# Keys by seven block products for two groups at a time, query products in front of the outputs, one probability buffer

## The chip, the cores and the metric

The kernel runs on one core of a Trainium2 chip. The metric is device time in microseconds (us) of one execution. Five engines work side by side, each with its own instruction queue: TensorE (PE) multiplies matrices into the accumulators (PSUM, 8 banks of 128 x 512 float32), VectorE (DVE) and ScalarE (ACT) do arithmetic and can read PSUM, GpSimd (POOL) does arithmetic on the working memory, and SyncE (SP) issues the transfers (DMA).

## The reference

Four sequences of 256 tokens, 512 features each, go through a half-weighted gated network, causal attention over a window of 128 tokens, and the same half-weighted network again:

```python
x = x + 0.5 * ffn(layernorm(x))
x = x + attention(layernorm(x))
x = x + 0.5 * ffn(layernorm(x))

def attention(x):                       # 32 query heads, 8 key heads, 128 wide
    q = rope(x @ wq); k = rope(x @ wk); v = x @ wv
    scores = q @ k.T / sqrt(128), only where (j <= i) & (j > i - 128)
    return (softmax(scores) @ v) @ wo   # four query heads share one key head
```

`ffn` is a 512 x 512 base product plus the outputs of the best two of eight small experts (16 wide). All is float32.

## The kernel before

**Halves, groups, units.** The 1024 tokens are treated in two halves `h` of two sequences (512 tokens). In each half the attention loop runs over eight groups `g`, one key head with its four query heads, and in each group over the two sequences `b`. One pass `(h, g, b)` is called a unit; there are 32. The loop is software-pipelined: in a unit the outputs of the unit before are formed, the transposes and values of this unit, the scores of the next unit, and keys, queries and values for the next group (or pair of groups).

**Products by blocks.** Queries (`queries`) and outputs (`outputs`) are not plain products. The weights and the tokens are cut into two by two blocks, some sums of blocks are made beforehand, and seven block products take the place of eight, with some additions after them. The names `a11` ... `s4` are blocks and sums on one side, `b11` ... `t4` on the other. `sums_a` and `sums_b` make them on POOL (four operations each; some in place), `sum_weights` for the query weights `wqs`, `sum_o_weights` for the output weights `wos`, `outputs` for the attention result `oTs`. `sum_tokens` makes the sums `xs` of the normalized tokens `xa` on DVE, once in a half. In `queries` every product fills one PSUM bank (two times 256 columns, two matmuls each); products 2, 3 and 4 add to banks that 1, 5 and 7 left. The sums between them (`p1c` copied by ACT, `u2`, `v1` and the sums into banks by DVE) use tiles with one slot each.

**Keys and values.** `keys` computes one group's keys by `project`: four matmuls of 512 columns (all tokens of the half) into one bank, and then `rope`, which is three DVE products and one POOL addition. `project_v` makes the values of two groups together, one tile of 128 tokens in a unit.

**Scores and probabilities.** `scores` puts the scores of one unit into three banks and takes the maxima on DVE; `exponentials` runs eight exponentials on ACT into a buffer `probs[b]`, one of two; `normalize` divides on POOL; `transposes` brings the probabilities into the layout that `values` multiplies with.

**PSUM.** Two tags with four banks each: "mm" for queries, keys, values, outputs and attention results, "s" for scores and transposes.

**The order.** A planner orders the instructions of PE, DVE and SP: it prefers the order in which they are written, but takes a later one where an earlier one, by its own estimate, isn't ready. From line 703 on, POOL and ACT keep the written order exactly. Every wait between engines is set by the framework, from the tiles that instructions read and write and the slots that they need.

**One unit as written** (loop from line 708): keys of the next group if b = 1; a tile of values; `normalize`; the outputs of the unit before (`late`, products in the order 4, 1 and 6, 2 and 3, 7 and 5, one bank for each); if b = 0 `sum_o_weights` and the first six steps of the next group's queries, if b = 1 `sum_weights` for the group after; `transposes`; the last two steps of the queries; the scores of the next unit; `values`; the exponentials of the next unit; and the four token sums of `outputs` for this unit. The loads of `load_qk` (keys double-buffered, queries in one slot) are written behind the queries. The table `loose` drops steps of the second network into the last eight units of the loop.

## Time and profile before

| what | value |
|---|---|
| median of 3 runs | 792.85 us (792.47 to 793.61) |
| the profiled execution | 793.98 us; its span 792.3 us, granted TensorE clock 1.000 |
| one group, two units, in the middle of a half (297.0 to 339.4) | 42.4 us; busy: PE 42.40, PEld 34.18, DVE 25.60, ACT 10.37, POOL 26.31 |
| `L374`, keys: matmuls | 128 records of 128x512, 57.5 us busy |
| `L400`, queries: matmuls | 896 records of 128x256 in four groups of rows |
| `L581`, outputs: matmuls | 868 records of 128x256 |
| POOL `L114` 128x256 / 128x512 | 738 ns / 1272 ns |
| DVE `L597` 128x256 / 128x512 out of PSUM | 405 ns / 691 ns |
| load of `wk` for one group | 256 KB, 2.7 us to landing, 16 of them |

PE and PEld are TensorE's matmuls and its weight loads, which overlap. A row of a timeline gives the start, the length, the engine and line, what is written from what, the shape, and how many instructions are merged. A row of waits gives who waited for whom, the total, how many times and the longest. Float32 matmuls leave two records each.

### The profile page before, as it was taken

To read this page: it belongs to the slowest core of one execution; us is meant where nothing else is said; L and a number is where in the kernel's file an instruction comes from. 1 tells how busy PE (TensorE), PEld (TensorE's weight loads), DVE (VectorE), ACT (ScalarE), POOL (GpSimd) and SP (SyncE) were. 2 spreads that over 40 slices of the span, in tenths; PEclk is the share of its full clock that TensorE was granted. 3 is DMA by queue.
4 is the path that set the end of the run, shared out by engine and by line. 5 is a ranking of instruction groups with operands and counts; after the bars stand their busy time and mean duration, and the time that the engine had idled before them with its cause. 6 is when DMAs were issued, how large, how long until landed. Compare 5 with 4: busy or idle time off the path is not lost.

```text
span 792.3 us, 10145 instructions
## 1 busy us (share of the span) xinstructions
PE 780.0 (98%) x3524; PEld 602.6 (76%) x3524; DVE 486.6 (61%) x1226; ACT 222.1 (28%) x766; POOL 451.4 (57%) x461
## 2 busy tenths in 40 slices
PE   6999999999999999999999999999999999999998
PEld 4557878787878888787878787878788787877654
DVE  4558563838474756659487728484757557574663
ACT  4342333222213140312222232213141412223331
POOL 5421775674747474757575665747474756653521
PEclk9999999999999999999999999999999999999999
DMA  8400221212021302112121212020303021100001
GB/s 294 158 1 19 76 67 53 93 54 67 8 99 41 106 14 91 57 53 67 54 95 53 67 54 88 23 95 9 106 14 101 20 58 49 54 1 26 1 27 54
DMA packets 33555, 48.90 MB, mean 62 GB/s; under 512 B 1248, under 2 KB 14304, under 8 KB 33504
## 3 DMA queue, kind: packets, MB, share of 16 engines
q1 hardware_dynamic: 33504, 48.26, 18.6%
q8 instruction: 28, 0.46, 0.2%
q14 instruction: 23, 0.19, 0.1%
HBM read 46.15 MB, written 2.10 MB: 61 GB/s over the span
## 4 chain that ended last, share of the span: by engine, by line
PE 96%; DMA 1%; DVE 1%; ACT 1%; SPq 0%; POOL 0%; issue 0%; DVEq 0%; ACTq 0%
PE q L400 24%; PE y L581 23%; PE pv L465 7%; PE ob L555 7%; PE pp_k L374 7%; PE po_f L330 6%; PE sb L497 5%; PE sa L482 4%; PE t L533 4%; PE oa L555 3%; PE pa_f L317 2%; PE po_f L342 1%; DMA x<-in_x_dram 1%; PE y L620 1%; PE pt_f L246 1%; ACT probs L515 0%
## 5 line engine op out<-in xcount | busy, mean ns | idle before, releaser
L369 POOL TENSOR_TENSOR qT<-ra_q,rb_q 128x512 f32<-128x512 f32 x64 | 81.4, 1272 | 154.9 <-DVE rb_q L365 154.9
L581 PE MATMUL y<-wo,oT 128*128 128x256 f32 x368 | 94.8, 379 | 0.0
L365 DVE TENSOR_TENSOR rb_q<-q,sin_sb 64x512 f32<-64x512 f32 x128 | 88.1, 688 | 1.7
L597 DVE TENSOR_TENSOR x<-y,x 128x256 f32<-128x256 f32 (+1 forms) x62 | 34.0, 548 | 83.0 <-PE y L581 82.9
L114 POOL TENSOR_TENSOR oTs<-oT 128x256 f32<-128x256 f32 x62 | 45.8, 738 | 59.7 <-ACT oT L558 57.2
L581 PEld LDWEIGHTS y<-wo,oT 128*128 128x128 f32 x368 | 69.8, 190 | 9.4
L537 ACT COPY p<-t 128x512 f32<-128x512 f32 x32 | 18.8, 586 | 203.1 <-PE t L533 203.1
L524 POOL TENSOR_TENSOR probs<-probs,sm 128x512 f32<-128x512 f32 x64 | 66.2, 1055 | 1.2 <-DVE sm L519 1.2
L581 PE MATMUL y<-wos,oTs 128*128 128x256 f32 x248 | 63.9, 380 | 0.6 <-POOL oTs L114 0.6
L465 PEld LDWEIGHTS pv<-wv,xa 128*128 128x128 f32 x256 | 48.6, 190 | 18.1 <-issue 12.9
L400 PE MATMUL q<-xa,wq 128*128 128x256 f32 x256 | 60.8, 379 | 0.0
L400 PE MATMUL q<-xs,wqs 128*128 128x256 f32 x256 | 60.6, 379 | 0.0
L400 PE MATMUL q<-xs,wq 128*128 128x256 f32 x256 | 60.5, 379 | 0.0
L555 PE MATMUL ob<-p,v 128*128 128x512 f32 x128 | 60.1, 592 | 0.0
L465 PE MATMUL pv<-wv,xa 128*128 128x256 f32 x256 | 60.0, 379 | 0.0
L330 PE MATMUL po_f<-wb_sb,xn_f 128*128 128x512 f32 x128 | 57.9, 594 | 0.0
L374 PE MATMUL pp_k<-xa,wk 128*128 128x512 f32 x128 | 57.5, 592 | 0.0
L590 DVE TENSOR_TENSOR z<-y,z 128x512 f32<-128x512 f32 x46 | 31.7, 690 | 40.2 <-PE y L581 40.2
L515 ACT ACTIVATE probs<-probs,nm 128x64 f32<-128x64 f32 (+1 forms) x128 | 46.3, 364 | 35.7 <-DVE nm L511 30.2
L400 PEld LDWEIGHTS q<-xa,wq 128*128 128x128 f32 x256 | 48.5, 190 | 6.9 <-issue 0.2
L400 PEld LDWEIGHTS q<-xs,wqs 128*128 128x128 f32 x256 | 48.6, 190 | 6.6
L581 PEld LDWEIGHTS y<-wos,oTs 128*128 128x128 f32 x248 | 46.9, 190 | 7.5 <-POOL oTs L114 1.0
(142 smaller groups left out, 1489.2 us busy)
## 6 DMA issues: line engine op xcount, KB each, us to landing
wq<-in_wq_dram SPq DMA_DIRECT2D x16, 1024.0 KB, 5.4
wo<-in_wo_dram SPq DMA_DIRECT2D x16, 1024.0 KB, 5.3
wk<-in_wk_dram SPq DMA_DIRECT2D x16, 256.0 KB, 2.7
wv<-in_wv_dram SPq DMA_DIRECT2D x8, 512.0 KB, 3.5
x<-in_x_dram SPq DMA_DIRECT2D x8, 256.0 KB, 7.2
out_dram<-x SPq DMA_DIRECT2D x8, 256.0 KB, 2.0
wb_sb<-in_w_base_dram SPq DMA_DIRECT2D x1, 1024.0 KB, 7.8
ar_sb<-in_w_ar_dram SPq DMA_DIRECT2D x1, 272.0 KB, 4.8
```

Of the source, the lines that this page charges most:

```text
L114: nc.gpsimd.tensor_tensor(dst, p, q, op)
L330: nc.tensor.matmul(po[i], x_of(i, c), wb_sb[:, c, :], start=(c == 0), stop=False)
L365: nc.vector.tensor_tensor(twice(b[o : o + half, :]), twice(src[i : i + half, :]), angle(sin_sb[o : o + half, :]), ALU.mult,)
L369: nc.gpsimd.tensor_tensor(dst, view(a), view(b), ALU.add)
L374: nc.tensor.matmul(pp, w[:, c, :], xa[h][:, c, :], start=(c == 0), stop=(c == KC - 1))
L400: nc.tensor.matmul(bank[:, ts(j, S)], w[:, c, ts(j, HD)], x[:, c, :], start=(new and j == 0 and c == 0), stop=(c == 1), skip_group_check=True,
L465: nc.tensor.matmul(pv[:, : 2 * HD], xa[h][:, c, ts(i, P)], weights["v", h, g][:, c, :], start=(c == 0), stop=(c == KC - 1),)
L497: nc.tensor.matmul(pb[:, ts(e, 3 * BLK)], q[:, 2 + e, 2 * p : 2 * p + 2, :], k[:, n - P : n + BLK], start=True, stop=True,)
L515: nc.scalar.activation(pr[:, n, :keys_of], src[:, :keys_of], AF.Exp, bias=nm[:, n : n + 1], scale=scale, accum_out=sm[:, n : n + 1],)
L524: nc.gpsimd.tensor_tensor(w, w, sm[:, n : n + G].unsqueeze(2).to_broadcast([P, G, P]), ALU.mult)
L555: nc.tensor.matmul(po, v[:, 2 * b + n, cols], part, start=(n == 0), stop=(n == len(parts) - 1))
L581: nc.tensor.matmul(py[:, ts(i, D // 2)], lhs[n - 1][:, c, :], weights["os", h, g][n - 1][:, c, :], start=(i == 0 and c == 0), stop=(c == 1 ...
```

## The change

`load_qk` is cut in two. `load_k` loads the key weights of two groups (512 KB) into one slot, `load_q` the queries' as before. `sum_weights` gets a kind, and makes block sums of key weights too. `keys` computes the keys of groups g and g + 1 at once: the rows of blocks are the two heads, the columns the two sequences, so that block c11 is head g for the first sequence, c12 head g for the second, and c21 and c22 are head g + 1. Two banks hold the four blocks, two blocks in each. It is called in the prologue for groups 0 and 1, and then in every second b = 1 unit. In a b = 0 unit all eight query steps are written in front of the outputs of the unit before; keys too now stand behind the values' tile and in front of the outputs. `probs` is one buffer. The loads change places as shown.

```diff
@@ -88,12 +88,18 @@
 
     weights = {}
 
-    def load_qk(h, g):
-        wk_g = sb.tile([P, KC, HD], F32, tag="wk", name=f"wk_{h}_{g}")
-        nc.sync.dma_start(out=wk_g, in_=wk[:, ts(g, HD)].rearrange("(c p) f -> p c f", p=P))
+    def load_k(h, g):
+
+        wk_g = sb.tile([P, KC, 2 * HD], F32, tag="wk", bufs=1, name=f"wk_{h}_{g}")
+        nc.sync.dma_start(
+            out=wk_g, in_=wk[:, ts(g // 2, 2 * HD)].rearrange("(c p) f -> p c f", p=P)
+        )
+        weights["k", h, g] = wk_g
+
+    def load_q(h, g):
         wq_g = sb.tile([P, KC, G * HD], F32, tag="wq", bufs=1, name=f"wq_{h}_{g}")
         nc.sync.dma_start(out=wq_g, in_=wq[:, ts(g, G * HD)].rearrange("(c p) f -> p c f", p=P))
-        weights["k", h, g], weights["q", h, g] = wk_g, wq_g
+        weights["q", h, g] = wq_g
 
     def load_v(h, g):
         wv_g = sb.tile([P, KC, 2 * HD], F32, tag="wv", name=f"wv_{h}_{g}")
@@ -119,13 +125,14 @@
             nc.gpsimd.tensor_tensor(dst, p, q, ALU.subtract)
         return b11, b21, b22, t4, t1, t2, t3
 
-    def sum_weights(h, g):
-
-        w = weights["q", h, g]
-        new = sb.tile([P, 3, 2, 2 * HD], F32, tag="wqs", bufs=1, name=f"wqs_{h}_{g}")
-        weights["qs", h, g] = sums_a(
-            w[:, :2, : 2 * HD], w[:, 2:, : 2 * HD], w[:, :2, 2 * HD :], w[:, 2:, 2 * HD :],
-            *(new[:, i] for i in range(3)),
+    def sum_weights(kind, h, g):
+
+
+        w = weights[kind, h, g]
+        n = w.shape[-1] // 2
+        new = sb.tile([P, 3, 2, n], F32, tag=f"w{kind}s", bufs=1, name=f"w{kind}s_{h}_{g}")
+        weights[kind + "s", h, g] = sums_a(
+            w[:, :2, :n], w[:, 2:, :n], w[:, :2, n:], w[:, 2:, n:], *(new[:, i] for i in range(3))
         )
 
     def load_o(h, g):
@@ -189,10 +196,8 @@
     by_heads(pick, fill_pick)
 
 
-    probs = []
-    for n in range(2):
-        probs.append(const.tile([P, 2 * G, P], F32, name=f"probs{n}"))
-        nc.gpsimd.memset(probs[n][:, :G:2, BLK:], 0.0)
+    probs = const.tile([P, 2 * G, P], F32, name="probs")
+    nc.gpsimd.memset(probs[:, :G:2, BLK:], 0.0)
     picked = pick.bitcast(mybir.dt.int32).rearrange("p (c k) -> p c k", k=BLK)
 
 
@@ -368,12 +373,6 @@
             )
         nc.gpsimd.tensor_tensor(dst, view(a), view(b), ALU.add)
 
-    def project(dst, w, h, name):
-        pp = mm_bank(f"pp_{name}")
-        for c in range(KC):
-            nc.tensor.matmul(pp, w[:, c, :], xa[h][:, c, :], start=(c == 0), stop=(c == KC - 1))
-        rope(dst, pp, name)
-
     def sum_tokens(h):
 
         sums = sb.tile([P, 4, 2, S], F32, tag="xs", bufs=1, name=f"xs_{h}")
@@ -382,6 +381,12 @@
         for dst, p, q in ((t1, b12, b11), (t2, b22, t1), (t3, b22, b12), (t4, b21, t2)):
             nc.vector.tensor_tensor(dst, p, q, ALU.subtract)
         xs[h] = (b11, b21, b22, t4, t1, t2, t3)
+
+    def add(dst, bank, other):
+        nc.vector.tensor_tensor(dst, bank, other, ALU.add)
+
+    def temp(name, at):
+        return sb.tile([HD, TH], F32, tag=name, bufs=1, name=f"{name}_{at}")
 
     def queries(h, g):
 
@@ -403,29 +408,23 @@
                     )
             return bank
 
-        def temp(name):
-            return sb.tile([HD, TH], F32, tag=name, bufs=1, name=f"{name}_{h}_{g}")
-
         def turn(b, j, src):
             rope(
                 qT[h, g][:, b, :, j : j + 2, :], src, f"q_{h}_{g}_{b}_{j}",
                 lambda t: t.rearrange("p (j e q) -> p e j q", j=2, q=BLK),
             )
 
-        def add(dst, bank, other):
-            nc.vector.tensor_tensor(dst, bank, other, ALU.add)
-
         def first():
             state["p1"] = product(1)
-            state["p1c"] = temp("p1c")
+            state["p1c"] = temp("p1c", f"q_{h}_{g}")
             nc.scalar.copy(state["p1c"], state["p1"])
 
         def sixth():
-            state["p6"], state["u2"] = product(6), temp("u2")
+            state["p6"], state["u2"] = product(6), temp("u2", f"q_{h}_{g}")
             add(state["u2"], state["p6"], state["p1c"])
 
         def fifth():
-            state["p5"], state["v1"] = product(5), temp("v1")
+            state["p5"], state["v1"] = product(5), temp("v1", f"q_{h}_{g}")
             add(state["v1"], state["p5"], state["u2"])
 
 
@@ -453,8 +452,36 @@
         return [first, sixth, fifth, seventh, second, third, turn_third, fourth]
 
     def keys(h, g):
-        kT[h, g] = sb.tile([HD, TH], F32, tag="kT", name=f"kT_{h}_{g}")
-        project(kT[h, g], weights["k", h, g], h, f"k_{h}_{g}")
+
+        x, w = xs[h], weights["ks", h, g]
+        banks = [mm_bank(f"k{n}_{h}_{g}").rearrange("p (b s) -> p b s", b=BPH) for n in range(2)]
+        (c11, c12), (c21, c22) = ((bank[:, 0, :], bank[:, 1, :]) for bank in banks)
+        p1c, u2, v1 = (temp(n, f"k_{h}_{g}")[:, :S] for n in ("p1c", "u2", "v1"))
+
+        def product(n, dst, start=False):
+            for c in range(2):
+                nc.tensor.matmul(
+                    dst, w[n - 1][:, c, :], x[n - 1][:, c, :],
+                    start=(start and c == 0), stop=(c == 1), skip_group_check=True,
+                )
+
+        for i in range(2):
+            kT[h, g + i] = sb.tile([HD, TH], F32, tag="kT", name=f"kT_{h}_{g + i}")
+        product(1, c11, True)
+        nc.scalar.copy(p1c, c11)
+        product(6, c22, True)
+        add(u2, c22, p1c)
+        product(5, c12)
+        add(v1, c12, u2)
+        product(7, c21)
+        add(c22, c21, v1)
+        product(2, c11)
+        product(3, c12)
+        add(c12, c12, u2)
+        rope(kT[h, g], banks[0].rearrange("p b s -> p (b s)"), f"k_{h}_{g}")
+        product(4, c21)
+        add(c21, c21, u2)
+        rope(kT[h, g + 1], banks[1].rearrange("p b s -> p (b s)"), f"k_{h}_{g + 1}")
 
     def project_v(h, g, i):
 
@@ -472,7 +499,7 @@
     def scores(h, g, b):
         o = b * S
         q, k = qT[h, g][:, b], kT[h, g]
-        pr = probs[b]
+        pr = probs
         mx = sb.tile([P, 2 * G], F32, tag="mx", bufs=3, name=f"mx_{h}_{g}_{b}")
         sm = sb.tile([P, 2 * G], F32, tag="sm", bufs=3, name=f"sm_{h}_{g}_{b}")
         pa = score_bank(f"sa_{h}_{g}_{b}").rearrange("p (c k) -> p c k", k=P)
@@ -625,7 +652,8 @@
 
     groups = [(h, g) for h in range(NHALF) for g in range(NKV)]
     units = [(h, g, b) for h, g in groups for b in range(BPH)]
-    load_qk(*groups[0])
+    load_k(*groups[0])
+    load_q(*groups[0])
     load_v(*groups[0])
     load_o(*groups[0])
     xa = [None] * NHALF
@@ -666,17 +694,18 @@
             halves[h](step)
     norm_attn(behind.popleft())
     sum_tokens(0)
-    sum_weights(*groups[0])
+    sum_weights("k", *groups[0])
+    sum_weights("q", *groups[0])
     keys(*groups[0])
+    load_k(*groups[2])
     for step in queries(*groups[0]):
         step()
-    load_qk(*groups[1])
-    sum_weights(*groups[1])
+    load_q(*groups[1])
+    sum_weights("q", *groups[1])
     for i in range(TPH):
         project_v(0, 0, i)
     load_v(*groups[2])
     load_o(*groups[1])
-
 
 
 
@@ -708,37 +737,37 @@
     for u, (h, g, b) in enumerate(units):
         n = groups.index((h, g)) + 1
         left = len(units) - u
-        rest = []
-        if b == 1 and n < len(groups):
-            keys(*groups[n])
         at = n + n % 2
         if at < len(groups):
             project_v(*groups[at], 2 * (1 - n % 2) + b)
         normalize(ahead[0], ahead[2])
         fill(left, 0)
+        if b == 0 and n < len(groups):
+            for step in queries(*groups[n]):
+                step()
+            if n % 2 == 0:
+                sum_weights("k", *groups[n])
+        elif b == 1 and n % 2 == 0 and n < len(groups):
+            keys(*groups[n])
+            if n + 2 < len(groups):
+                load_k(*groups[n + 2])
         run(late, len(late))
         if b == 0:
             sum_o_weights(h, g)
-            if n < len(groups):
-                if n > 1:
-                    load_o(*groups[n])
-                rest = queries(*groups[n])
-                while len(rest) > 2:
-                    rest.pop(0)()
+            if n + 1 < len(groups):
+                load_q(*groups[n + 1])
+            if 1 < n < len(groups):
+                load_o(*groups[n])
         else:
             if g == NKV - 2 and h + 1 < NHALF:
                 sum_tokens(h + 1)
             if n + 1 < len(groups):
-                sum_weights(*groups[n + 1])
+                sum_weights("q", *groups[n + 1])
                 if n % 2 == 0 and n + 2 < len(groups):
                     load_v(*groups[n + 2])
         fill(left, 1)
         p0, p1 = transposes(h, g, b, ahead[0])
-        for step in rest:
-            step()
         fill(left, 2)
-        if b == 0 and n + 1 < len(groups):
-            load_qk(*groups[n + 1])
         if left > 1:
             ahead = scores(*units[u + 1])
         oT = values(h, g, b, p0, p1)
```

## The prediction

> **What bounds the kernel.** I read the page's busy times first, then its chain of waits, then the waits of TensorE alone, then TensorE's timeline through one group.
>
> ```profile
> PE 780.0 (98%) x3524; PEld 602.6 (76%) x3524; DVE 486.6 (61%) x1226; ACT 222.1 (28%) x766; POOL 451.4 (57%) x461
> ...
> PE 96%; DMA 1%; DVE 1%; ACT 1%; SPq 0%; POOL 0%; issue 0%; DVEq 0%; ACTq 0%
> ```
>
> TensorE (PE) holds 96% of the chain that ended last. Its waits (us in total, times, longest) come to 8.3 us, 7.5 of them at tile transposes, nearly all in one wait of 6.4:
>
> ```profile
> PE pt_f L246 <- ACT xc_f L235: 7.5, 2, 6.4
> PE y L581 <- POOL oTs L114: 0.6, 1, 0.6
> PE po_f L342 <- ACT ht_f L338: 0.2, 1, 0.2
> ```
>
> So in the group loop PE never stops: a matmul taken out of its stream is saved in full, and a stall put into it is paid in full. The timeline (start, length, count at the end) of one b = 1 unit:
>
> ```profile
> 315.21 1.02 PE L555 MATMUL oa<-p,v 128*128 128x512 f32 x2
> 316.07 1.88 PE L555 MATMUL ob<-p,v 128*128 128x512 f32 x4
> 317.79 3.60 PE L374 MATMUL pp_k<-xa,wk 128*128 128x512 f32 x8
> 321.22 1.89 PE L465 MATMUL pv<-wv,xa 128*128 128x256 f32 x8
> 322.95 1.03 PE L581 MATMUL y<-wos,oT 128*128 128x256 f32 x4
> 323.81 1.03 PE L581 MATMUL y<-wo,oT 128*128 128x256 f32 x4
> ```
>
> Read starts, not lengths (ends are modelled). Each float32 matmul leaves two records. Eight of 512 columns take 321.22 − 317.79 = 3.43 us, 0.429 each; eight of 256 columns take 1.73 us, 0.216 each. Half the columns cost half, plus 1.5 ns.
>
> **1. The products.** Two groups of keys take 16 records × 0.429 = 6.86 us now. The seven products are 7 × 2 matmuls × 2 = 28 records × 0.216 = 6.05 us. Gain 0.81 us a pair, and 8 pairs: **−6.5 us**.
> A rule speaks against this: the Trainium skill, "Trainium Kernel Development and Optimization", Performance Expectations, judges TensorE by weight-load busy time, not by matmul busy time. The change adds 12 loads a pair, 96 × 0.190 = 18 us, so PEld goes from 76% to about 79%. If that load were exposed, the sum would be +11.7 us. The row decides: a load of 190 ns already lies under each 256-column record spaced 216 ns apart, so I count it at nothing; only 26 ns of cover is left.
>
> **2. New side work a pair.** POOL: four 128x256 sums (row L114, 738 ns), 3.0 us. DVE: five 128x256 adds from PSUM (row L597, 405 ns), 2.0 us. ACT: one 128x256 copy (row L469, 368 ns). Over 8 pairs that is 24, 16 and 3 us, on engines busy 57, 61 and 28%: nothing by itself. What counts is where PE waits for it.
>
> **3. Unit lengths.** Take a unit's first pv matmul as 0. By the timeline's steps pv is 1.73, queries 7 × 1.73 = 12.1, outputs 6.05, transposes 0.87, scores 2.2, values 2.6. In the new order a b = 0 unit is 25.5 us: pv, queries to 13.8, outputs to 19.9, transposes to 20.7. A b = 1 unit is 13.4 us without keys, and 19.5 with them (next group even).
>
> **4. Does the key chain stall PE?** Each product must be answered in the 0.86 us of the next one: 0.2 us from PE to DVE or ACT (y ending near 337.23, its add starting at 337.43), 0.4 for the add, 0.1 back. That fits if the engine is free. ACT isn't:
>
> ```profile
> 335.32 0.35 ACT L515 ACTIVATE probs<-probs,nm 128x64 f32<-128x64 f32 x1
> ...
> 338.04 0.20 ACT L515 ACTIVATION_READ_ACCUMULATOR probs<-sb,nm 128x1 f32 x1
> 338.13 0.37 ACT L469 COPY v<-pv 128x256 f32<-128x256 f32 x1
> ```
>
> This unit began at 334.64, so exponentials hold ACT to 3.5 and the pv copy to 3.9. ACT keeps written order, so the key chain's first copy ends near 4.3. The fifth product would start at 1.73 + 2 × 0.86 = 3.45; it writes the other half of the bank that this copy reads. The Trainium skill, "PSUM — Partial Sum Buffer", section "PSUM bank collisions raise a hardware error", says to guard PSUM by bank, not by address. By address nothing waits: 0. By bank the wait is 0.85 us × 7 pairs in the loop = 6.0 us, nearly the whole gain. No row shows two engines on halves of one bank. I take the bank rule, but expect the planner to put other matmuls into the hole (the raw output products, 0.86 us each, are ready). It does such things now: near the end it moved transposes ahead of the last output products, leaving under 0.1 us:
>
> ```profile
> 749.87 1.03 PE L581 MATMUL y<-wo,oTs 128*128 128x256 f32 x4
> 750.73 1.04 PE L533 MATMUL t<-ident,probs 128*128 128x128 f32 x8
> 751.68 1.13 PE L581 MATMUL y<-wos,oTs 128*128 128x256 f32 x4
> ```
>
> Cost between 0 and 6.0, taken near 0.
>
> **5. Queries in front of outputs.** All four "mm" banks hold query sums, and outputs now follow at once (today transposes stand before the last product, scores after it). DVE frees the banks. Measured on the timeline from the first query product (300.06): adds start at 3.7, 5.4 and 7.1, ropes run 7.9 to 12.2, then both adds of u2 in 1.3 us. Today the masks push these back; in the new order they follow directly, and the last two ropes (2.1 us each) end at 15.5 and 17.7. Output banks are wanted at 12.1, 13.0, 14.7 and 16.4. The third gets its bank 1.0 us late, the fourth then 0.4 late: up to 1.4 × 14 loop units = 19 us. Movable work lies next: transposes (0.87), then scores (0.89). I take 1 us for the whole loop here. What makes up for it: the rope backlog now drains under the outputs rather than under the masks and maxima that follow transposes (today DVE gets to the scores at 318.86, 3.7 us after PE ended them).
>
> **6. POOL order.** `sum_o_weights` starts when the outputs release `wos`: today at 7.8 in a b = 0 unit, then at 19.9 to 20.9. It takes 4 × 1.345 = 5.4 us, ending at most 0.8 into the next unit, where outputs need it at 1.7 in a unit without keys. Then come four sums of 0.80 each, as now (335.50 to 338.6), so product 6 keeps the thin margin that it has today before b = 0 outputs. Normalization ends at about 6.1 (340.65 − 334.64); transposes now come at 7.8 without the keys as a cushion. Margins of 1 us and 1.7 us: nothing, but if outputs slip by another 1 us, product 6 waits some 0.6 in 8 units. Where `sum_weights("k")` lies in front (3.2 us), the next unit has 6 us of keys as cover.
>
> **7. One probability buffer.** Its writers wait for the transposes of the last unit, which already stand before scores in PE's order: 0. It removes an option, no wait.
>
> **8. Loads.** SP issues half as many key loads of twice the size, freed by the keys, wanted over one unit (25 us) later against 2.7 to 3.5 us to land. The query load moves ahead of the output load, which stands behind outputs now ending 12 us later; landing at about 27, it is wanted a unit later. 0.
>
> **9. The first group.** Keys now need DVE answers at 60 to 67 us, when DVE has half 1's updates and statistics; the query chain shares one-slot temporaries (p1c, u2, v1) with it and follows only after the last key add. Between −0.5 (earlier ropes) and +3; PE still has the query products and transposes to fill with, so +1.0.
>
> **Sum.** −6.5 + 1.0 + 1.0 = −4.5 us on the profiled run (span 792.3, run 793.98, so 1.7 us around it). That run is 1.1 over the median of 792.85; taking the difference from the median: **788.4 us**. Its own range is 785.8 (no stall at all, and a little more) to 791.
>
> **Rivals.**
> *The exponentials eat the gain (14%).* The hole of part 4 isn't filled: +6.0, about 792.5 with part of the other stalls. For it: ACT's order is fixed, and each of 7 pairs meets it. Against: planner's moves above.
> *PSUM banks decide (14%), the slower side.* The third and fourth output products after queries wait for the last two ropes; paid in full +19.5 in place of 1: about 807; half paid, 797. It decides once about a third of it stays unfilled (6.5 us). For it: DVE would be busy from 3.7 to nearly the unit's end. Against: filler of 1.8 us stands next.
> *POOL becomes the answerer (9%).* Outputs' end, weight sums, token sums, product 6 in a row: 0.6 to 1.6 us × 8 units, 793 to 801.
> *It doesn't do what it says (1%)*: keys are plain to see in the edit; 792.9.
>
> **Chances.** Forecast 62%. Below 0.2% (1.6 us) a measurement of this kernel can't tell a change. Faster: the forecast plus a few mild rivals, 0.66; same 0.12, mainly the first rival; slower 0.22, the others. The range runs 785.8 to 796: the first rival and the mild ends of the others are in, full bank waits left out.
>
> **What would show it.** Right: no pp_k group; key products at 0.216 a record, 6.05 us a pair; PE waits still under 10 us; PE idle-free between queries and outputs, perhaps with transposes moved between. Wrong: PE waits on DVE q or ACT p1c in units with keys (part 4), on DVE rb_q or y at outputs after queries (5), on POOL oTs or wos (6), or a gap around 60 to 70 us (9). Key records spaced well above 216 ns would break part 1.

## The result, and the profile after

The changed kernel takes 819.23 us (median of 6 runs, 818.51 to 820.84) against 793.36 us of the kernel before on the same chip (6 runs, 792.47 to 793.62): a ratio of 1.033, interval 1.0317 to 1.0343. It is 3.3% slower. The forecast was 788.4 us and the range ended at 796. The profiled execution of the changed kernel took 820.07 us, its span 818.2.

The page of the changed kernel (busy times; granted clock in 40 slices; chain that ended last):

```profile
PE 786.0 (96%) x3620; PEld 622.8 (76%) x3620; DVE 517.4 (63%) x1266; ACT 221.2 (27%) x774; POOL 473.4 (58%) x492
...
PEclk9999899999999999999999999999999999999999
...
PE 74%; DVE 13%; POOL 7%; issue 3%; DMA 1%; ACT 1%; SPq 0%; DVEq 0%; POOLq 0%; ACTq 0%
```

TensorE held 96% of the chain before and holds 74% now; VectorE and POOL have 20% together. The clock has one slice that was not there before, the fifth. The table of TensorE's waits (us in total, times, longest) names places:

```profile
PE y L608 <- DVE rb_q L370: 9.1, 15, 1.2
PE pt_f L251 <- ACT xc_f L240: 6.6, 1, 6.6
PE sa L509 <- POOL qT L374: 4.0, 1, 4.0
PE ob L582 <- DVE p L569: 2.3, 1, 2.3
PE y L608 <- POOL wos L125: 2.2, 1, 2.2
PE ph_f L341 <- POOL hl_f L290: 1.4, 1, 1.4
```

The second row is the kernel before's one large wait. The first has 15 members: one in each of 13 units that have queries in front of outputs, and two in the last such unit. The others fall once each: `hl_f` and `qT` at the start, `p` and `wos` around the first unit.

**A ledger by units.** Waits name only a part of 26 us. A sharper reading takes the first matmul of `values` in each unit (`oa`) and sets its start in the changed kernel against its start in the kernel before. A row says by how much the difference grows over a stretch; a unit's stretch runs from the `oa` of the unit before to its own:

| stretch | difference (us) |
|---|---|
| up to the `oa` of the first unit, (0,0,0) | +13.1, of which 2.6 is the second key head, computed there now |
| from there to the next `oa`, with the outputs of the first unit | +2.2, though it lost 3.4 us of keys |
| each of 14 later b = 0 units | +0.73 to +1.00, the last +2.3; sum +14.3 |
| a b = 1 unit with keys, and the next b = 1 unit without | +2.61 and −3.43: −0.82 a pair, in five of seven pairs; the other two −0.3 and +0.8 |
| all from the second unit to the last | +10.7 |
| whole loop and start | +26.0 |

So the products pay what was worked out, to 0.01 us a pair, in the five pairs that no other wait touches. Two other things bury it: the start with the first unit, some 16 us over what the work there needs (10.5 up to the first `oa`, 13.1 − 2.6, and 5.6 behind it, 2.2 + 3.4), and about one microsecond in every later unit that has queries.

A b = 0 unit shows the second. TensorE's timeline of the changed kernel, behind a set of queries (start, length, work, count, and in brackets a recorded wait):

```profile
325.14 1.03 PE L608 MATMUL y<-wos,oTs 128*128 128x256 f32 x4
326.01 0.49 PE L560 MATMUL t<-ident,probs 128*128 128x128 f32 x3
327.00 1.10 PE L608 MATMUL y<-wo,oT 128*128 128x256 f32 x4 [0.50 <-DVE rb_q L370]
327.93 1.03 PE L608 MATMUL y<-wo,oTs 128*128 128x256 f32 x4
328.80 0.38 PE L560 MATMUL t<-ident,probs 128*128 128x128 f32 x2
329.12 1.10 PE L608 MATMUL y<-wos,oTs 128*128 128x256 f32 x4
```

The planner did what was hoped for: it pulled transposes (`t`) into the hole where an output product lacks a bank. But only three records at a time, and from the first output (323.42) to the scores (331.25) the unit takes 7.83 us, where seven products of 0.864 and eight transposes in 0.87 make 6.92. Of the 0.91 us lost, 0.50 is a recorded wait; the rest lies at the switches between transposes and products. The scores come only behind the last output product.

The key chain, on the other hand, runs without a stall:

```profile
337.75 1.03 PE L463 MATMUL k<-xa,wk 128*128 128x256 f32 x4
338.61 1.03 PE L463 MATMUL k<-xs,wks 128*128 128x256 f32 x4
339.48 1.03 PE L608 MATMUL y<-wos,oT 128*128 128x256 f32 x4
340.34 1.03 PE L463 MATMUL k<-xs,wk 128*128 128x256 f32 x4
```

The third row is an output product, put where product 5 was expected to wait for the copy of product 1; the starts stay 0.86 us apart.

### The profile page after: what moved, and what is told of

The parts are those of the page before. It is cut to its first block, busy times and chain, and to the rows that moved or that the text cites. A ratio compares the mean times of both kernels' runs of the same rounds, so it can differ in the third digit from the quotient of the medians.

```text
span 818.2 us, 10473 instructions
## 1 busy us (share of the span) xinstructions
PE 786.0 (96%) x3620; PEld 622.8 (76%) x3620; DVE 517.4 (63%) x1266; ACT 221.2 (27%) x774; POOL 473.4 (58%) x492
## 4 chain that ended last, share of the span: by engine, by line
PE 74%; DVE 13%; POOL 7%; issue 3%; DMA 1%; ACT 1%; SPq 0%; DVEq 0%; POOLq 0%; ACTq 0%
PE y L608 18%; PE q L405 13%; DVE rb_q L370 8%; PE ob L582 7%; PE k L463 6%; PE pv L492 6%; PE sb L524 5%; PE po_f L335 5%; PE sa L509 3%; PE oa L582 3%; POOL qT L374 3%; DVE ra_q L368 3%; PE t L560 3%; PE po_f L347 2%; PE pa_f L322 1%
## 5 line engine op out<-in xcount | busy, mean ns | idle before, releaser
L492 PEld LDWEIGHTS pv<-wv,xa 128*128 128x128 f32 x256 | 49.7, 194 | 19.2 <-issue 13.4
L546 DVE RECIPROCAL sm<-sm 128x8 f32<-128x8 f32 x32 | 6.5, 202 | 91.2 <-ACT probs L542 91.2
L492 PE MATMUL pv<-wv,xa 128*128 128x256 f32 x256 | 61.8, 386 | 0.0
L405 PEld LDWEIGHTS q<-xs,wq 128*128 128x128 f32 x256 | 48.6, 190 | 6.7
L374 POOL TENSOR_TENSOR kT<-ra_k,rb_k 128x512 f32<-128x512 f32 x16 | 20.3, 1271 | 53.6 <-DVE rb_k L370 53.6
```

What stands on the lines that cost most here:

```text
L374: nc.gpsimd.tensor_tensor(dst, view(a), view(b), ALU.add)
L405: nc.tensor.matmul(bank[:, ts(j, S)], w[:, c, ts(j, HD)], x[:, c, :], start=(new and j == 0 and c == 0), stop=(c == 1), skip_group_check=True,
L492: nc.tensor.matmul(pv[:, : 2 * HD], xa[h][:, c, ts(i, P)], weights["v", h, g][:, c, :], start=(c == 0), stop=(c == KC - 1),)
```

## The experiments

The theory was: (a) the products give 0.8 us a pair; (b) queries in front of outputs cost about 1 us in each unit that has them, because output products wait for PSUM banks; (c) the start costs the rest, because the first keys now need key sums, VectorE and POOL at the wrong time. The rivals: the key chain stalls (so that taking keys out of the change would mend it), or POOL decides the loop. In the edits, `...` stands for lines left out. All times are medians beside runs of the kernel before on the same chip (792.79 to 793.48 in the various sets).

**One part of the change alone.** First the query move by itself, in the kernel before:

```diff
         normalize(ahead[0], ahead[2])
         fill(left, 0)
+        if b == 0 and n < len(groups):
+            for step in queries(*groups[n]):
+                step()
         run(late, len(late))
...
-                rest = queries(*groups[n])
-                while len(rest) > 2:
-                    rest.pop(0)()
...
-        for step in rest:
-            step()
```

> The kernel before with one thing of the change: all eight query steps in front of the outputs (plain keys, two probability buffers). Theory A (query banks: in every b = 0 unit outputs wait for the last ropes to free their PSUM banks, 0.95 us a unit): 793.4 + 14 = about 807, with PE waiting for DVE rb_q at some 14 output products. Rival B (the seven-product key chain is what costs in the loop): 793.4, no such waits.

Measured: 810.96 us, ratio 1.0227 (1.0212 to 1.0242). The move costs 18.0 us in a kernel that has no new keys at all. Its table of waits has the same row:

```profile
PE y L581 <- DVE rb_q L365: 9.5, 15, 1.2
```

By the ledger 15.0 us fall in the 14 later units with queries: that is (b). Another 4.3 fall behind the first `oa`, and 1.2 are gained before it. So the loss of the first unit comes with the move of the queries too, not with the keys.

Then the keys by themselves: the changed kernel with the query steps back behind the outputs, and the key sums behind the last of them.

```diff
-        if b == 0 and n < len(groups):
-            for step in queries(*groups[n]):
-                step()
...
+            if n < len(groups):
+                rest = queries(*groups[n])
+                while len(rest) > 2:
+                    rest.pop(0)()
...
+        for step in rest:
+            step()
+        if b == 0 and n < len(groups) and n % 2 == 0:
+            sum_weights("k", *groups[n])
...
```

> The changed kernel with the queries back behind the outputs, where they stood before; the seven-product keys and the one probability buffer stay. Theory A: the 14 us of bank waits go and the late start of the loop (about 15 us) stays: about 804. Rival B (key chain): no gain, 817 to 820.

Measured: 857.29 us, 1.0814 (1.0796 to 1.0832), at a granted clock of 0.978. This was a miss: without the query move the keys are much worse, not better. TensorE's waits in this kernel:

```profile
PE y L608 <- POOL oTs L120: 20.9, 15, 2.3
PE k L463 <- POOL wks L120: 13.3, 7, 1.9
```

Both are POOL's. Its key sums (`wks`) stand behind the rope additions of the queries and come too late for product 6. The token sums (`oTs`) stand in POOL's fixed order behind rope additions too: those of the queries in a b = 1 unit, where every second unit has also lost the 3.4 us of keys that lay in front of the outputs, and those of two keys and then four query-weight sums in the b = 0 unit after keys. They are wanted before they are done. The query move is then more than a change of place: with it `oTs` costs 0.9 us in place of 20.9, and by itself the move costs 18 us.

**The first keys.** Plain products for the first two groups in the prologue, no key sums there:

```diff
+    def keys_plain(h, g):
+        for i in range(2):
+            kT[h, g + i] = sb.tile([HD, TH], F32, tag="kT", name=f"kT_{h}_{g + i}")
+            pp = mm_bank(f"pp_k_{h}_{g + i}")
+            for c in range(KC):
+                nc.tensor.matmul(
+                    pp, weights["k", h, g][:, c, ts(i, HD)], xa[h][:, c, :],
+                    start=(c == 0), stop=(c == KC - 1),
+                )
+            rope(kT[h, g + i], pp, f"k_{h}_{g + i}")
...
-    sum_weights("k", *groups[0])
...
-    keys(*groups[0])
+    keys_plain(*groups[0])
```

> The changed kernel with plain products for the first two groups' keys alone (two banks, eight matmuls of 512 columns; no key weight sums at the start). Theory C (at the start the key chain delays the queries' DVE work by 8.6 us through shared temporaries and a busy DVE; TensorE idles and its clock drops): scores of the first unit some 10 us earlier, about 807. Rival D (the start is late because of the queries in front of the outputs of the first unit): 817 or more.

Measured: 809.56 us, 1.0208 (1.0193 to 1.0223): 9.7 us less than the change, although the products themselves now cost 0.8 more. The waits `sa` for `qT` and `ph_f` for `hl_f` are gone from the table, and the clock is 1.000. Up to the first `oa` the ledger reads +2.7 for 3.4 us of added keys, so the whole loss of 10.5 us in front of the loop is gone; the stretch behind it keeps its +2.2. Both edits together:

> Both repairs in one: queries behind the outputs and plain keys for the first two groups; seven products remain for seven pairs. If A and C are the whole of it: 793.4 - 7 x 0.81 = 787.7, allow 787 to 791. If the key chain itself costs in the loop: 793 or more. If only one of A and C holds: 802 to 806.

Measured: 843.97 us, 1.0652 (1.0634 to 1.067), clock 0.986: 13.3 us under keys_only, with both POOL rows as they were (21.2 and 13.4 us). This was a miss as well, for the same reason. The start and the loop are in the main separate costs.

**What in the start.** In the changed kernel, the first scores of the loop:

```profile
90.19 0.61 PE L509 MATMUL sa<-kT,qT 128*128 128x64 f32 x4
94.77 1.22 PE L509 MATMUL sa<-kT,qT 128*128 128x64 f32 x4 [3.97 <-POOL qT L374]
95.78 2.77 PE L524 MATMUL sb<-kT,qT 128*128 128x192 f32 x8
```

and POOL's timeline before that point:

```profile
88.32 1.27 POOL L374 TENSOR_TENSOR qT<-ra_q,rb_q 128x512 f32<-128x512 f32 x1 [2.18 <-DVE rb_q L370]
89.55 1.27 POOL L120 TENSOR_TENSOR wqs<-wq 128x512 f32<-128x512 f32 x1
90.90 1.26 POOL L120 TENSOR_TENSOR wq<-wq 128x512 f32<-128x512 f32 x1
92.23 1.26 POOL L120 TENSOR_TENSOR wqs<-wq 128x512 f32<-128x512 f32 x1
93.45 1.26 POOL L374 TENSOR_TENSOR qT<-ra_q,rb_q 128x512 f32<-128x512 f32 x1
```

TensorE waits 3.97 us for the last rope addition, and three sums for the *next* group's queries stand in front of that addition. They got there because VectorE is late: its first query addition (`u_q`) starts at 77.71 here and at 69.13 in the kernel before, behind half 1's statistics and then the whole key chain. The wait also costs afterwards: `sb` starts 95.78 and `pv` follows at 98.34, 2.56 us for work that took 1.30 in the kernel before (85.29 to 86.59).

Three edits ask which of these matters. A temporary of its own for the key chain (is it the shared slot?):

```diff
-        p1c, u2, v1 = (temp(n, f"k_{h}_{g}")[:, :S] for n in ("p1c", "u2", "v1"))
+        p1c, u2, v1 = (
+            sb.tile([HD, S], F32, tag="u2k", bufs=1, name=f"u2_k_{h}_{g}") if n == "u2"
+            else temp(n, f"k_{h}_{g}")[:, :S] for n in ("p1c", "u2", "v1")
+        )
```

> The changed kernel with a slot of its own for the keys' u2, so that the first queries' u2 needn't wait for the last key addition. Theory C1 (the shared temporary holds up the first group's queries): scores of the first unit several us earlier, 810 to 814. Rival C2 (DVE is simply busy with half 1 and then with the key ropes, in order): no more than 2 us, 817 to 819.

Measured: 818.87 us, 1.0326 (1.0311 to 1.0341). No effect: not the slot of `u2` (those of `p1c` and `v1` stayed shared).

The next group's query sums written behind everything else in the prologue:

```diff
     load_q(*groups[1])
-    sum_weights("q", *groups[1])
...
+    sum_weights("q", *groups[1])
```

> The changed kernel with the block sums of the second group's query weights written just before the loop, so that POOL makes them after the first group's last rope additions and not between them. Theory C3 (4 us of TensorE idling and 3 us of lowered clock at the first scores come from POOL's order there): the 4.0 us wait of sa for POOL qT goes and the clock stays up, about 812. If the wait only moves on (probabilities of the first unit late): 817 to 819.

Measured: 818.19 us, 1.0322 (1.0306 to 1.0337). POOL's order came out as it was: in the prologue the planner still orders POOL, and took the sums early again. The run says nothing for or against. So the written order was forced on POOL there (the same lines, set in):

```diff
+    with tc.manual_schedule(engines={mybir.EngineType.Pool}):
         keys(*groups[0])
         load_k(*groups[2])
         for step in queries(*groups[0]):
             step()
         load_q(*groups[1])
         sum_weights("q", *groups[1])
```

> The changed kernel with POOL's order fixed as written at the start too, so that the first group's last rope addition stands before the sums of the second group's query weights (the order of ropes_before_sums came out unchanged). Theory C3: the 4.0 us wait of sa for POOL qT falls to about 1, the clock stays up (3 us): about 813. Rival: 817 to 819.

Measured: 812.62 us, 1.025 (1.0236 to 1.0264). The wait for `qT` falls from 4.0 to 1.0, the wait for `wos` from 2.2 to 0.5, and the time falls by 6.6 us: 4.7 of recorded waits, and the dip in the clock, which is gone from the page. In the ledger of the profiled runs the stretch up to the first `oa` gets 7.7 us shorter (+5.5 for +13.1). This order on POOL is then most of the 10.5 us lost in front of the loop, though not of the 16: the +2.2 behind the first `oa` stays. A part of the remainder is the wait of 1.4 us for `hl_f`, which POOL makes from routing weights of VectorE. POOL idled in front of it, for VectorE: the key sums (`wks`, 21.08 to 24.22) push the query sums later, until 29.47, and beside them VectorE's small routing operations take up to 1.30 us where they take 0.19 afterwards (the last section shows why).

**What in the loop.** If output products lack banks, either another bank or other work in the hole must help. One bank from the scores to "mm":

```diff
-        return ps.tile([P, 512], F32, tag="mm", bufs=4, name=name)
+        return ps.tile([P, 512], F32, tag="mm", bufs=5, name=name)
...
-        return ps.tile([P, 512], F32, tag="s", bufs=4, name=name)
+        return ps.tile([P, 512], F32, tag="s", bufs=3, name=name)
...
```

> The changed kernel with five PSUM banks for sums and three for scores and transposes (four and four before). Theory A (a free bank is what the outputs behind the queries wait for): the 15 waits for DVE rb_q, 9.1 us, and the transposes cut into pieces go; 819 - 13 = about 806, unless three score banks bring a wait of their own. If DVE or POOL results and not banks were awaited: 819.

Measured: 808.94 us, 1.0208 (1.0187 to 1.0229), waits now:

```profile
PE ob L582 <- DVE p L569: 3.5, 2, 3.0
PE sb L524 <- DVE p L569: 2.0, 3, 1.1
...
PE y L608 <- DVE rb_q L370: 1.1, 1, 1.1
```

The bank waits for `rb_q` went from 15 to 1, and 10.3 us with them; three score banks ask some of it back. The other way is the tile of values, 1.73 us of TensorE work, between queries and outputs in b = 0 units:

```diff
-        if at < len(groups):
+        if at < len(groups) and b == 1:
             project_v(*groups[at], 2 * (1 - n % 2) + b)
...
             for step in queries(*groups[n]):
                 step()
+            if at < len(groups):
+                project_v(*groups[at], 2 * (1 - n % 2) + b)
```

> The changed kernel with the b = 0 unit's tile of values written behind the queries rather than in front of them: 1.73 us of TensorE work whose bank ACT frees in 0.6 us, put where the outputs wait for banks. Theory A: the same gain by other means, the waits for DVE rb_q fall from 9.1 us to under 2, about 806. If it isn't the banks: 819.

Measured: 808.65 us, 1.0186 (1.0163 to 1.0209): 10.6 us less, `rb_q` down to 2.9 us in 4 waits. An ordinary b = 0 unit is 25.5 us again, the figure of the kernel before. (b) is shown from both sides.

And with queries behind the outputs, is the rest POOL's? The key sums in front of the rope additions:

```diff
+            if n % 2 == 0 and n < len(groups):
+                sum_weights("k", *groups[n])
             if n < len(groups):
                 rest = queries(*groups[n])
...
-        if b == 0 and n < len(groups) and n % 2 == 0:
-            sum_weights("k", *groups[n])
```

> keys_behind_plain_first with the key weight sums written in front of the queries' rope additions, so that the second key product needn't wait for them. Theory E (POOL's order: the rope additions, late behind the masks, stand in front of the four token sums, and units without keys no longer have 3.4 us of key products as cover): the 13.4 us of waits for POOL wks go, the 21 us for POOL oTs stay; 844 - 16 = about 825 to 830. If the key weight sums were all of it: about 800 or less.

Measured: 822.78 us, 1.0377 (1.0362 to 1.0391), against 843.97: the waits for `wks` (13.4 us) are gone and 21 us with them, as the granted clock of the profiled run rose from 0.986 to 0.998. The other row stays:

```profile
PE y L619 <- POOL oTs L120: 21.2, 15, 2.3
```

So by these waits POOL decides in the old order, and the new order was the way round that. No run took the `oTs` waits out of the old order.

**A version that keeps the products and drops the costs.** Plain keys at the start, the values' tile between, the first unit's `wos` sums ahead of its queries:

```diff
+        if u == 0:
+            sum_o_weights(h, g)
...
-            sum_o_weights(h, g)
+            if u > 0:
+                sum_o_weights(h, g)
```

> All repairs in the order of the change: plain keys for the first two groups, the b = 0 unit's values between queries and outputs, and in the first unit the output weight sums in front of the queries' rope additions on POOL. From plain_first (809.6) the bank waits go (what values_between_only gained, 10 to 11 us) and some 4 us of the first unit's waits for DVE p and POOL wos: 788 to 796. If the seven-product keys are worth their 7 x 0.81 = 5.7 us in the loop: under 793; if not, it stays at 793 or above.

Measured: 796.17 us, 1.0042 (1.0028 to 1.0055): 23 of the 26 us are back, 4.8 of them behind the first `oa`. By what was expected this would speak against the products (793 or more); the ledger shows where their gain went, into four units that carry extra steps, at 1.5 to 2.3 us each. The statistics of the second network and the token sums of the second half were moved:

```diff
-        8: ("0M0 0M1 1M0 1M1", "", ""), 5: ("0X0 0X1", "", ""), 4: ("0T0 0T1 0A0 0A1 0R", "", ""),
+        8: ("", "0M0 0M1 1M0 1M1", ""), 5: ("0X0 0X1", "", ""), 4: ("0T0 0T1", "0R", "", "0A0 0A1"),
...
-            if g == NKV - 2 and h + 1 < NHALF:
-                sum_tokens(h + 1)
...
+        if b == 1 and g == NKV - 2 and h + 1 < NHALF:
+            sum_tokens(h + 1)
```

Here the gate products `A0 A1` take the place between queries and outputs in the one unit that has no values left, and the routing `R` a later one.

> values_between with three writings moved: the second half's token sums behind the values of their unit (there DVE's 3.5 us held up the masks, 1.7 us), the moments of the last network behind the outputs (1.5 us of bank waits in unit (1,4,0)), and in unit (1,6,0), where no tile of values is left, the small products of the last network behind the queries as filler (2.3 us). If these three places are what keeps values_between from its 5.7 us: 796.2 - 5.5 = 790.7, allow 789 to 793. If the waits move on: 795 to 797.

Measured: 795.22 us, 1.003 (1.002 to 1.0039). The routing (twelve small VectorE operations up to the masks) now stood in front of VectorE's masked weights `p`, and TensorE waited 2.3 us there. So `0R` went one place further:

```diff
-4: ("0T0 0T1", "0R", "", "0A0 0A1"),
-3: ("", "0B0 0B1", "0G 1X0 1X1")
+4: ("0T0 0T1", "", "", "0A0 0A1"),
+3: ("0R", "0B0 0B1", "0G 1X0 1X1")
```

> The kernel mended, with the routing (R) of the next group taken from the place before the last keyless unit's masks to the start of that unit's successor list (one place later), so that its VectorE operations no longer stand in front of that unit's masks. If the key products' 0.82 us a pair is real in a whole kernel and the 2.35 us wait of the outputs for VectorE's masked weights in the second-last loop unit (with some 1 us of ScalarE evictions beside it) is all that still hides it: 795.2 - 3.5 = about 791.5 us (790.5 to 793), under the kernel before. If waits only move on to another unit, because VectorE's routing work has to lie somewhere: 794.5 to 796, and the gain of the products stays hidden in this order of steps.

Measured: 793.86 us, 1.0018 (1.0009 to 1.0027). A miss of both expectations: VectorE's order hardly changed (the planner drew the routing forward to the old place, where its inputs are ready), and the wait stayed:

```profile
699.12 1.99 PE L593 MATMUL ob<-p,v 128*128 128x512 f32 x4 [2.33 <-DVE p L580]
701.87 1.10 PE L619 MATMUL y<-wos,oT 128*128 128x256 f32 x4 [0.77 <-ACT oT L596]
```

The median of 16 runs is lower by 1.4 us than in the run of mended, but the profiled spans differ by 0.5 only, and the runs of both kernels spread over 4 to 5 us, in part with the granted clock (last section); no gain of this edit is claimed. The planner can't start the routing before its gate product. So the second gate product went a unit later, and the routing behind it:

```diff
-4: ("0T0 0T1", "", "", "0A0 0A1"),
-3: ("0R", "0B0 0B1", "0G 1X0 1X1")
+4: ("0T0 0T1", "", "", "0A0"),
+3: ("0A1", "0R 0B0 0B1", "0G 1X0 1X1")
```

> As mended_late_routing, but the second of the two gate products (A1) and with it the routing (R), which cannot start before it, go one unit later: A0 stays between queries and outputs (0.95 us, enough for the bank wait there), A1 stands in front of the next unit's outputs, where TensorE now waits for ScalarE's and POOL's work on the attention result (0.77 and 0.36 us), R behind them. Since the routing's operations now hang on a later result, the planner cannot draw them in front of VectorE's masks. If the key products' gain is real in a whole kernel and this 2.33 us wait with those two is what still hides it: 793.9 - 3.4 = about 790.5 us (789.5 to 792), under the kernel before. If waits only move (to the gate's transposes behind the later routing): 793 to 795.

Measured: 790.77 us (5 runs, 789.66 to 790.85) against 793.48: a ratio of 0.9963, interval 0.9949 to 0.9976. This kernel beats both. The same stretch of TensorE's timeline has no wait left but one of 0.35:

```profile
697.43 1.88 PE L593 MATMUL ob<-p,v 128*128 128x512 f32 x4
699.15 1.09 PE L322 MATMUL pa_f<-ar_sb,xn_f 128*128 128x136 f32 x8
700.08 1.10 PE L619 MATMUL y<-wos,oT 128*128 128x256 f32 x4
```

The gate product (`pa_f`) fills the time in which the outputs waited for ScalarE. But this kernel holds moved steps as well as the key products. The last run takes the products alone out of it:

```diff
-            if n % 2 == 0:
-                sum_weights("k", *groups[n])
         elif b == 1 and n % 2 == 0 and n < len(groups):
-            keys(*groups[n])
+            keys_plain(*groups[n])
```

> As mended_late_gate, with the keys of each pair of groups by plain products again (two groups by four matmuls of 512 columns, at the same place) and no sums of key weights; all else unchanged. If the block products for the keys are worth in a whole kernel what they are worth between single units, this takes 7 pairs x 0.82 = 5.7 us more than mended_late_gate: about 796.5 us (795.5 to 797.5), above the kernel before. If the gain of mended_late_gate over the kernel before comes from the moved steps and not from the key products: 790 to 792.

Measured: 796.1 us (6 runs, 795.51 to 796.5) against 793.21, ratio 1.0033 (1.0021 to 1.0045). The edit takes the sums of key weights on POOL away too. The `oa` in front of one pair of keys and the one behind it, first in mended_late_gate, then here:

```profile
399.31 1.02 PE L593 MATMUL oa<-p,v 128*128 128x512 f32 x2
418.77 1.02 PE L593 MATMUL oa<-p,v 128*128 128x512 f32 x2
...
401.96 1.02 PE L593 MATMUL oa<-p,v 128*128 128x512 f32 x2
422.24 1.02 PE L593 MATMUL oa<-p,v 128*128 128x512 f32 x2
```

The stretch takes 19.46 us with block products and 20.28 with plain ones, and so it goes at every pair of keys: 0.82 us, seven times, 5.9 us at the end with the little that the start adds. The spans are 794.6 and 788.7, and the medians, taken on two chips, differ by 5.3 (their ratios to the kernel before by 5.6 us). So the key products are worth in a whole kernel what they are worth in a unit, and the rest of the change, with the moved steps, costs about 2.9 us against the kernel before.

## Why the prediction was wrong

The sum was off by 30.5 us on the profiled runs (−4.5 forecast, +26.0 measured). By the ledger 13.3 of it belong to step 5, 9.5 to step 9, 5.6 to the first unit, and 2.1 to the two pairs of keys whose gain was lost where TensorE also waited for ScalarE or POOL.

**Right.** Step 1: 0.81 us a pair was forecast and 0.82 measured, seven times over, in mended_late_gate against late_gate_plain_keys; the first pair, at the start, was not measured by itself. The rule on weight loads, which spoke against it, did not bear on the time: mended_late_gate has 84 more loads than late_gate_plain_keys and 14 us more of load time, and it is the faster one. Step 2: nothing by itself. Step 3: the unit lengths stand as worked out wherever no bank wait falls (25.5 and 13.4 us). Step 4: the hole in the key chain was filled, cost 0. That the framework makes product 5 wait by bank, and not by address, shows in banks53: at the start there it stands directly behind product 1 and waits 0.46 us for the copy out of the other half of its bank. Steps 7 and 8: no wait for the one buffer or for a load in the table.

**Wrong: step 5, by far the larger part in the loop.** The mechanism, the engine, the place and the bound were right: up to 1.4 us a unit, 19 us. Even the times were: the last two ropes were to end 15.5 and 17.7 us after the first query product, and in the unit shown above the two late outputs start at 15.7 and 17.8 (327.00 and 329.12, from 311.33). The step failed where it said "I take 1 us for the whole loop". Measured is 14.3 us over 14 units in the changed kernel, and 15.0 in the same units with the move alone. The filler was there, and the transposes were used; but three of them filled 0.3 us of the first hole, 0.5 us of it stayed open, the switches cost some more, and the scores were not drawn forward. The forecast set 1.8 us of movable work against 1.4 us of waits as if either could be poured into the other. The second rival ("PSUM banks decide") is the one that came true; 14% was too little for a mechanism whose bound was three times the gain.

**Wrong: step 9.** "So +1.0", from a range of −0.5 to +3. Measured: 10.5 us over what the work up to the first `oa` needs, all of it gone with plain keys there. The step saw that VectorE has half 1's work at that time. It did not follow the lateness on to POOL, whose rope addition then fell behind three sums (4.0 us), and it gave no price to the clock.

**Wrong: step 6, in the first unit only.** "Nothing" for the margins of `sum_o_weights` holds in the loop of the changed kernel. In the first unit no outputs of an earlier unit stand between the queries and the next work of TensorE, and so it comes too early: `wos` cost 2.2 us and VectorE's masks 2.3, of 5.6 in all. With these sums ahead of the rope additions and the values' tile moved (values_between), 0.9 of it is left. As for the third rival, POOL did not become the answerer in the order that was chosen, and did in the order that was not (20.9 us of waits in keys_only).

**Left open.** In mended_late_gate one wait of 1.4 us for VectorE's `p` remains in unit (0,6,0), beside the token sums; it was not tried. How the 10.5 us in front of the loop divide between waits, clock and later work is shown only as far as plain_first and pool_in_order_first go, and what decides whether a wait lowers the clock is not shown.

## What to carry to other kernels

When a move puts a producer of full PSUM banks directly in front of a consumer of banks, price the bank waits at their bound unless one whole piece of other work, longer than the wait, can be written between them; a tile of values of 1.73 us mended what 1.8 us of transposes in pieces did not. Before forecasting a move as free, ask also what the old place was buying: here queries behind outputs kept banks apart but held POOL's additions, and either order had a price of about 20 us (18.0 for the move alone, 20.9 of waits in keys_only) until other work was put between. And a stage that runs once, like the first group, deserves the same walk through every engine's queue as the loop, since one stall of 4 us there costs more than the gain of four pairs.

## What the runs showed of the hardware

**A stall can cost twice.** After some TensorE waits the matmuls behind run slower for a few us, though TensorE has full work. In keys_only, TensorE's timeline:

```profile
346.46 1.13 PE L463 MATMUL k<-xs,wks 128*128 128x256 f32 x4 [1.91 <-POOL wks L120]
347.43 1.52 PE L608 MATMUL y<-wos,oT 128*128 128x256 f32 x4
349.46 2.08 PE L608 MATMUL y<-wo,oT 128*128 128x256 f32 x4 [0.52 <-DVE x L624]
351.33 1.92 PE L608 MATMUL y<-wos,oTs 128*128 128x256 f32 x4
353.04 1.83 PE L463 MATMUL k<-xs,wk 128*128 128x256 f32 x4
354.70 1.03 PE L463 MATMUL k<-xs,wks 128*128 128x256 f32 x4
```

Four records of 256 columns take 1.03 us by the row, and 1.92 behind the two waits, until 354.70; the granted clock is 0.50 from 350 to 354 us, and 0.978 over the whole run. In the changed kernel it is 0.50 from 96 to 100 us, behind the 3.97 us wait, and 0.57 from 33.0 to 36.8, behind the 1.4 us wait for `hl_f`. The 0.5 us waits at the banks left it at 1.00 (319.5 to 344 us).

The length of a wait does not decide it alone. Of the seven waits of 1.9 us for `wks` in keys_only, four were followed by ten microseconds at a granted clock of 0.66 to 0.83, and three by 1.00. In the changed kernel two longer ones were followed by 1.00:

```profile
119.93 1.98 PE L582 MATMUL ob<-p,v 128*128 128x512 f32 x4 [2.32 <-DVE p L569]
125.88 1.13 PE L608 MATMUL y<-wos,oT 128*128 128x256 f32 x4 [2.24 <-POOL wos L125]
```

The times of a kernel spread accordingly. In mended_late_routing, which keeps one wait of 2.33 us, the ten runs with a clock of 0.999 or more took 792.4 to 794.8 us, the six with less 794.9 to 797.3. In mended_late_gate, where that wait is gone, all five runs have 0.999 or more and lie within 1.2 us.

**Small VectorE operations wait out POOL's.** In mended_late_routing, VectorE operations of 128x16 elements, of which the first and third read two inputs from the working memory:

```profile
691.85 1.19 DVE L272 SCALAR_TENSOR_TENSOR k_f<-l_f,rank 128x16 f32<-128x16 f32 x1
693.08 0.17 DVE L273 TENSOR_REDUCE r_f<-k_f 128x2 f32<-128x16 f32 x1
...
694.30 1.21 DVE L276 SCALAR_TENSOR_TENSOR l_f<-s_f,l_f 128x16 f32<-128x16 f32 x1
695.55 0.17 DVE L277 TENSOR_REDUCE m_f<-l_f 128x2 f32<-128x16 f32 x1
```

and POOL beside them:

```profile
691.73 2.51 POOL L327 TENSOR_TENSOR x<-x,half_bias 128x512 f32<-128x512 f32 x2
694.19 1.29 POOL L125 TENSOR_TENSOR wos<-wo 128x512 f32<-128x512 f32 x1
695.56 1.26 POOL L125 TENSOR_TENSOR wo<-wo 128x512 f32<-128x512 f32 x1
```

The two-input operations last 1.2 us and end where a POOL operation ends (695.51 beside 695.48, and four others also 0.03 us behind one); the one-input reductions between them take 0.17. The Trainium skill, "SBUF — State Buffer", section "SBUF: two separate sides", says that a VectorE operation with two inputs there and a POOL operation that reads there share a pair of ports, which one of them holds for its whole length. The trace agrees. It would explain how twelve operations, seven of them of 0.2 us, with two other additions between them, became a VectorE queue of 7 us (691.40 to 698.46) in front of the masks, and why the routing in the changed kernel's start was late. No run separated it from other causes.
